# Causal attention scores from 64 contraction rows per head, two heads at a time on the two halves of the PE array's rows

## The chip, the cores and the metric

One core of a Trainium2 chip runs the whole kernel. The time is device microseconds of that core; the kernel before took a median of 586.83 us over three runs (585.6 to 587.18). Where this text speaks of an engine: PE is the matrix engine, DVE the vector engine, ACT the scalar engine, POOL the general-purpose engine, SP the queue from which the transfers are issued.

## The reference

A batch of 256 tokens of 512 numbers goes through three layers, each added to its input:

```python
z = sigmoid((LN(x) Wq^T + bq) (ctx Wk^T + bk)^T / sqrt(128))   # 256 x 25088, no softmax
x = x + z (ctx Wv^T + bv)
c = LN(x) W_kv_down                                            # 256 x 128
k, v, q = heads(c W_k_up), heads(c W_v_up), heads(LN(x) W_q)   # 16 heads of 32
s = (q k^T + rot(LN(x) W_q_rope) rot(c W_k_rope)^T) / 8        # the rotary part is shared by all heads
x = x + concat(softmax(causal(s)) v) W_o
x = x + sum over 8 experts of one_hot * (relu(x wg)^2 * (x wu)) wd
```

The score of a head is thus a product over 64 numbers: 32 that belong to the head and 32 rotary ones that all heads share.

## The kernel before

The first layer streams 25088 context rows in 49 chunks; it takes the first 480 us or so of the span, and the change does not touch its code. What follows, called the section here, is written as small functions that are called in one hand-written list (from L582 on). The suffix or argument `tt` is the half of the tokens (0 or 1, 128 each), `u` a unit of scores, `P` is 128.

For each half: `N1` and `X` normalise and transpose the tokens; `QR` makes the rotary queries, `CKV` the compressed keys and values, `KR` the rotary keys, `K` the heads' keys, `VS` the values, `Q` (four parts) the heads' queries. `S` makes one unit of scores: the matmuls into one PSUM bank of 128x512, the causal mask added by a bf16 matmul with an identity, then a row maximum on DVE (`mx`) and one exponential per head on ACT (`pr`), which also sums the row. `PT` transposes a unit's weights on PE and copies them on DVE (`pt`), `PV` multiplies them with the values, `R1` and `R2` bring the reciprocal sums into shape, `AT` scales and splits, `WO` is the output projection; then `N2` and `Y` normalise and transpose for the experts, and `GU`, `GE`, `IT`, `DN` are the experts' steps.

The scores of two heads come from one matmul over all 128 rows. `kbd` holds the keys as a block pattern: the keys of head `j` of a group of four lie on rows 32j to 32j+31 of column block `j`, the rotary keys on the other half's rows, and the rest is zero, set by POOL (L307). `qs` holds two variants of the queries, each with one half of a group's heads on 64 rows and the rotary queries on the first 32 rows of the other half; it too is zeroed by POOL first (L581). For tt=0 a unit is one group of four heads (two matmuls of 256 columns); for tt=1 it is two heads (one matmul of 512 columns).

All of this is float32; a float32 matmul shows as two weight loads and two matmul records. The order on each engine is the order of the calls: `in_order` (L35) chains every PE, ACT, DVE and POOL instruction to the one before it on its engine, so that nothing is moved by a scheduler. Three buffer rings matter here: the banks of PSUM (`bank`, six), the buffers of the exponentials (`pr`, tag "wr", two) and those of the transposed weights (`pt`, tag "z", two).

Of the kernel before, what the change touches and what calls it, by code (L numbers as in the profile page):

```python
# [11 lines left out]
F32 = mybir.dt.float32  # L12
F32R = mybir.dt.float32r
BF16 = mybir.dt.bfloat16
AF = mybir.ActivationFunctionType
ALU = mybir.AluOpType
AX = mybir.AxisListType
# [3 lines left out]
P = 128  # L21
T = 256
D = 512
KD = D // P
# [24 lines left out]
def body(ctx, tc, a, out, nch=NCH):  # L49
    nc = tc.nc  # L50
    mm = nc.tensor.matmul
    copy, vcopy, tt2 = nc.scalar.copy, nc.vector.tensor_copy, nc.vector.tensor_tensor

    sm = ctx.enter_context(tc.tile_pool(name="sm", bufs=1))
    sb = ctx.enter_context(tc.tile_pool(name="sb", bufs=1))
# [19 lines left out]
    def bank(name):  # L75
        return psum.tile([P, D], F32, tag="b", name=name, bufs=6)
# [4 lines left out]
    def toks(t):  # L81
        return slice(t * P, (t + 1) * P)
# [30 lines left out]
    mask = sm.tile([P, P], BF16, name="mask")  # L113
# [3 lines left out]
    identb = sm.tile([P, P], BF16, name="identb")  # L117
# [25 lines left out]
    rT, rN, sT, sN, kp, zz = {}, {}, {}, {}, {}, {}  # L143
# [101 lines left out]
    ps = bank("qp_ps")[:, :T]  # L245
# [17 lines left out]
    for c in range(nch):  # L263
# [28 lines left out]
        if c >= 4 and plain:  # L292
            n = plain.pop()
# [8 lines left out]
    oh, ol = pair("o", [P, KD, T], "oh")  # L302
    xn = [None, None]

    kbd = [sb.tile([P, 2, 4, T], F32, tag="rT", name=f"kbd{i}", bufs=2) for i in range(2)]
    for i in range(2):
        nc.gpsimd.memset(kbd[i], 0.0)  # L307
    sums = sm.tile([P, 2, NH], F32, name="sums")


# [41 lines left out]
    def prod(ps, tt, w):  # L352
        for j in range(KD):
            mm(ps, lhsT=w(j), rhs=xT[tt][:, j, :], start=j == 0, stop=j == KD - 1)
# [7 lines left out]

    ckv, qr = [None] * 2, [None] * 2

    def CKV(tt):
        ps = bank(f"ckv_ps{tt}")[:, 0:P]
        prod(ps, tt, lambda j: pw["wkvd"][:, toks(j)])
        ckv[tt] = sb.tile([P, P], F32, name=f"ckv{tt}")
        copy(ckv[tt], ps)

    def QR(tt):
        ps = bank(f"qr_ps{tt}")[0:64, 0:P]
        prod(ps, tt, lambda j: pw["wqr"][:, 64 * j:64 * (j + 1)])
        qr[tt] = sb.tile([32, P], F32, name=f"qr{tt}")
        rotated("q", qr[tt], ps, tt)
        for i, r in enumerate((64, 0)):
            nc.vector.tensor_scalar(qs[r:r + 32, tt, i], qr[tt][:, None, :].broadcast_to([32, KD, P]), 0.125, None, ALU.mult)

    def KR(tt):
        ps = bank(f"kr_ps{tt}")[0:64, 0:P]  # L380
        mm(ps, lhsT=pw["wkr"], rhs=ckv[tt], start=True, stop=True)
        kr = sb.tile([32, P], F32, tag="kr", name=f"kr{tt}")
        rotated("k", kr, ps, tt)
        for r in (64, 0):
            for h in range(2):
                (vcopy if h else copy)(kbd[h][r:r + 32, :, 2 - r // 32:4 - r // 32, toks(tt)],
                                       kr[:, None, None, :].broadcast_to([32, 2, 2, P]))

    def K(tt):
        for h in range(2):  # L390
            ps = bank(f"k_ps{tt}{h}")[:, :2 * P].rearrange("p (g t) -> p g t", g=2)
            for g in range(2):
                mm(ps[:, g, :], lhsT=pw["wku"][:, toks(2 * h + g)], rhs=ckv[tt], start=True, stop=True)
            for j in range(4):
                r = slice(32 * j, 32 * j + 32)
                (vcopy if h else copy)(kbd[h][r, :, j, toks(tt)], ps[r])

    def VS(tt):
        ps = bank(f"vs_ps{tt}")
        mm(ps, lhsT=ckv[tt], rhs=pw["wvu"], start=True, stop=True)  # L400
        copy(vs[tt], ps)

    qps = [None, None]

    def Q(tt, g):
        if g == 0:
            qps[tt] = bank(f"q_ps{tt}").rearrange("p (g t) -> p g t", g=KD)
        prod(qps[tt][:, g, :], tt, lambda j: pw["wq2"][:, j * D + g * P:j * D + (g + 1) * P])
        if g == KD - 1:
            for i in range(2):  # L410
                r = slice(64 * i, 64 * i + 64)
                nc.scalar.activation(qs[r, tt, i], qps[tt][r], AF.Copy, scale=0.125)


    pv = [None, None]
    pr, pt = {}, {}

    def heads(tt, u):
        return (u, 0, 4) if tt == 0 else (u // 2, 2 * (u % 2), 2)

    def S(tt, u):
        g, h0, n = heads(tt, u)
        nk = P * (tt + 1)
        p3 = bank(f"s{tt}_{u}").rearrange("p (h k) -> p h k", h=n)
        if tt == 0:
            mm(p3, lhsT=identb, rhs=mask[:, None, :].broadcast_to([P, n, P]), start=True, stop=False)
        for h in range(h0, h0 + n, 2):
            mm(p3[:, h - h0:h - h0 + 2, :], lhsT=qs[:, tt, h // 2, g, :], rhs=kbd[g // 2][:, g % 2, h:h + 2, :nk],  # L428
               start=tt == 1, stop=tt == 0 and h == 2)
        if tt == 1:  # L430
            mm(p3[:, :, P:], lhsT=identb, rhs=mask[:, None, :].broadcast_to([P, n, P]), start=False, stop=True)
        mx = sm.tile([P, 4], F32, tag="mx", name=f"mx{tt}_{u}", bufs=4)
        nc.vector.tensor_reduce(mx[:, :n], p3, AX.X, ALU.max, negate=True)
        pr[tt, u] = sb.tile([P, D], F32, tag="wr", name=f"pr{tt}_{u}", bufs=2).rearrange("p (h k) -> p h k", h=n)
        for i in range(n):
            h = 4 * g + h0 + i
            nc.scalar.activation(pr[tt, u][:, i, :], p3[:, i, :], AF.Exp, bias=mx[:, i:i + 1],
                                 accum_out=sums[:, tt, h:h + 1])

    def PT(tt, u):  # L440
        n = heads(tt, u)[2]
        ps = bank(f"pt{tt}_{u}")
        for i in range(n):
            for kt in range(tt + 1):
                nc.tensor.transpose(ps[:, toks(i * (tt + 1) + kt)], pr[tt, u][:, i, toks(kt)], ident)  # L445
        pt[tt, u] = sb.tile([P, D], F32, tag="z", name=f"pt{tt}_{u}", bufs=2)
        vcopy(pt[tt, u], ps)

    def PV(tt, u):
        g, h0, n = heads(tt, u)  # L450
        if u == 0:
            pv[tt] = psum.tile([P, KD, P], F32, tag=f"acc{tt}", name=f"pv{tt}")
        for i in range(n):
            r = slice(32 * (h0 + i), 32 * (h0 + i + 1))
            for kt in range(tt + 1):
                mm(pv[tt][r, g, :], lhsT=vs[kt][:, g * P + r.start:g * P + r.stop],  # L456
                   rhs=pt[tt, u][:, toks(i * (tt + 1) + kt)], start=kt == 0, stop=kt == tt)
# [3 lines left out]
    def R1(tt):  # L461

        r = sm.tile([P, NH], F32, tag="r", name=f"r{tt}")
        nc.vector.reciprocal(r, sums[:, tt, :])
        rT2[tt] = tmp(f"rx{tt}")
        vcopy(rT2[tt].rearrange("p (h d) -> p h d", h=NH), r[:, :, None].broadcast_to([P, NH, 32]))
# [6 lines left out]
    def AT(tt):  # L473
        at = tmp(f"at{tt}").rearrange("p (g t) -> p g t", g=KD)
        tt2(at, pv[tt], rT2[tt], ALU.mult)
        att[tt] = [t.rearrange("p (g t) -> p g t", g=KD) for t in pair(f"at{tt}", [P, D], "at")]
        split(*att[tt], at)
# [13 lines left out]
    def Y(tt):  # L491
        ps = transposed(bank(f"xc_ps{tt}"), xn[tt])
        split(yhl[0][:, :, toks(tt)], yhl[1][:, :, toks(tt)], ps)
        yT[tt] = sb.tile([P, KD, P], F32, tag=f"xT{tt}", name=f"yT{tt}")
        copy(yT[tt], ps)
# [21 lines left out]
    def GU(tt, e, i, alone=False):  # L517
        if i == 0 or alone:
            gps[tt, e, i] = bank(f"gu{tt}_{e}_{i}").rearrange("p (e w) -> p e w", e=2)
        gps[tt, e, 1] = gps[tt, e, i]  # L520
        w = gu[e + i]
        for j in range(KD):
            s = slice(2 * j * P, 2 * (j + 1) * P)
            mm3(gps[tt, e, i][:, i, :], yhl[0][:, j, toks(tt)], yhl[1][:, j, toks(tt)], w[:, 0, s], w[:, 1, s],
                j == 0, j == KD - 1)
# [39 lines left out]
    ps = bank("rows_ps")  # L565
# [12 lines left out]
    AV1(len(late))  # L578
    o1 = O1(1)
    qs = sb.tile([P, 2, 2, KD, P], F32, tag="N0", name="qs", bufs=2)  # L580
    nc.gpsimd.memset(qs, 0.0)  # L581
    for e, tag in ((5, "N0"), (6, "N1"), (7, "N1")):  # L582
        load_gu(e, tag, 2)
    for e in range(4, E):
# [15 lines left out]
    for i in range(2):  # L600
        nc.sync.dma_start(f(wo[i]), spill["wo"][:, i * KD * D:(i + 1) * KD * D])
    S(0, 0)
    S(0, 1)
    QR(1)
    CKV(1)
    PT(0, 0)
    S(0, 2)
    KR(1)
    K(1)
    PV(0, 0)  # L610
    PT(0, 1)
    Q(1, 0)
    S(0, 3)
    Q(1, 1)
    R1(0)
    VS(1)
    PT(0, 2)
    PV(0, 1)
    PT(0, 3)
    Q(1, 2)  # L620
    Q(1, 3)
# [4 lines left out]
    PV(0, 3)  # L626
    R2(0)
    S(1, 0)
    S(1, 1)
    AT(0)  # L630
    S(1, 2)
    PT(1, 0)
    S(1, 3)
    PT(1, 1)
    WO(0)
    PV(1, 0)
    PV(1, 1)
    PT(1, 2)
    S(1, 4)
    S(1, 5)  # L640
    PV(1, 2)
    N2(0)
    PT(1, 3)
    S(1, 6)
    PT(1, 4)
    Y(0)
    S(1, 7)
    PV(1, 3)
    PV(1, 4)
    PT(1, 5)  # L650
    PT(1, 6)
    GU(0, 0, 0)
    PV(1, 5)
    PT(1, 7)
    R1(1)
    GU(0, 0, 1)
# [114 lines left out]
```

## Time and profile before

| | us |
|---|---|
| median of the timed runs | 586.83 |
| the profiled execution's own time | 586.28 |
| its span (first to last instruction) | 584.5 |
| PE busy | 570.6 (98%) |
| DVE busy | 459.7 (79%) |
| ACT busy | 395.1 (68%) |
| POOL busy | 21.1 (4%) |

The page of the profile lists busy time per engine, a picture of the span in 40 slices, the chain of work that ended last, and groups of instructions with their mean duration and the idle time ahead of them. The answers of the trace give single instructions in order of time. [...] the step from one start to the next says what it costs in a row of matmuls. Times within the run are microseconds from the start of the span.

### The profile page before, as it was taken

The page shows a single profiled execution, that of the slowest core. Times are in us where ns is not written, and L with a number is a line of the kernel's source. Part 1 is how long each engine was busy: PE and PEld are TensorE (multiplying, and loading weights), DVE is VectorE, ACT ScalarE, POOL GpSimd, SP SyncE. Part 2 cuts the span into 40 slices and gives each one's busy share as a digit, 9 for nine tenths or more (in the row PEclk, how much of TensorE's full clock was granted, in tenths as well). Part 3 has the DMA queues.
Part 4 walks back from the last instruction along what each step waited for, and adds up shares of the span by engine and source line. Part 5 has one row for each costly group of instructions (what it writes and reads, how often), then busy time and mean ns, then how long its engine had stood idle before and what let it go on. Part 6 is the DMA issues. An engine that isn't in the chain of part 4 may idle for free.

```text
span 584.5 us, 8061 instructions
## 1 busy us (share of the span) xinstructions
PE 570.6 (98%) x3036; PEld 481.7 (82%) x3036; DVE 459.7 (79%) x528; ACT 395.1 (68%) x512; POOL 21.1 (4%) x28
## 2 busy tenths in 40 slices
PE   4999999999999999999999999999999999999997
PEld 3888888888888888888888888888888887876996
DVE  6898888888888888888888888787878765667543
ACT  5877777777777777777777776767676752574211
POOL 5200000000000000000000000000000041000000
PEclk9999999999999999999999999999999999999999
DMA  8897887879888888788988887565657477700000
GB/s 288 334 368 283 278 295 281 321 278 317 287 324 276 325 271 325 266 337 298 332 282 319 274 337 245 208 225 206 234 198 243 149 295 262 316 1 1 1 1 36
DMA packets 33526, 144.94 MB, mean 248 GB/s; under 512 B 4240, under 2 KB 4432, under 8 KB 19792
## 3 DMA queue, kind: packets, MB, share of 16 engines
q1 hardware_dynamic: 33488, 144.44, 69.3%
q8 instruction: 23, 0.38, 0.2%
q14 instruction: 15, 0.12, 0.1%
HBM read 129.22 MB, written 15.20 MB: 247 GB/s over the span
## 4 chain that ended last, share of the span: by engine, by line
PE 95%; DVE 3%; DMA 1%; issue 0%; POOL 0%; ACT 0%; SPq 0%; POOLq 0%
PE acc L68 15%; PE acc L69 15%; PE acc L70 15%; PE kp_ps L70 8%; PE kp_ps L69 8%; PE kp_ps L68 8%; PE sc L70 4%; PE sc L69 4%; PE sc L68 4%; PE s L428 2%; PE gu L68 1%; PE gu L69 1%; PE gu L70 1%; PE pt L445 1%; DMA wq_r<-in_wq 1%; PE pv L456 1%
## 5 line engine op out<-in xcount | busy, mean ns | idle before, releaser
L68 PE MATMUL acc<-N,z 128*128 128x512 f32 x392 | 153.9, 393 | 0.0
L69 PE MATMUL acc<-N,z 128*128 128x512 f32 x392 | 153.7, 392 | 0.0
L65 DVE TENSOR_TENSOR N<-rN,N 128x2048 fp32r<-128x2048 f32 (+1 forms) x53 | 111.6, 2110 | 52.3 <-ACT N L64 52.2
L70 PE MATMUL acc<-N,z 128*128 128x512 f32 x392 | 152.5, 389 | 0.0
L65 DVE TENSOR_TENSOR T<-rT,T 128x2048 fp32r<-128x2048 f32 (+1 forms) x49 | 110.3, 2252 | 15.3 <-ACT T L64 15.3
L187 ACT ACTIVATE z<-sc 128x512 f32<-128x512 f32 x98 | 58.7, 599 | 66.5 <-PE sc L70 66.2
L64 ACT CAST N<-rN 128x2048 fp32r<-128x2048 f32 (+1 forms) x55 | 94.4, 1725 | 6.1
L64 ACT CAST T<-rT 128x2048 fp32r<-128x2048 f32 (+1 forms) x55 | 94.3, 1721 | 0.9 <-DMA rT<-in_ctxT 0.7
L70 PEld LDWEIGHTS acc<-N,z 128*128 128x128 f32 x392 | 73.6, 188 | 16.0
L68 PEld LDWEIGHTS acc<-N,z 128*128 128x128 f32 x392 | 74.0, 189 | 12.3
L69 PEld LDWEIGHTS acc<-N,z 128*128 128x128 f32 x392 | 74.0, 189 | 11.7
L68 PE MATMUL kp_ps<-T,wk 128*128 128x512 f32 x196 | 76.9, 392 | 0.0
L70 PE MATMUL kp_ps<-T,wk 128*128 128x512 f32 x196 | 76.7, 392 | 0.0
L69 PE MATMUL kp_ps<-T,wk 128*128 128x512 f32 x192 | 74.7, 389 | 0.0
L189 DVE TENSOR_TENSOR zacc<-zacc,z 128x512 f32<-128x512 f32 x98 | 67.2, 686 | 3.7 <-ACT z L187 1.7
L65 DVE TENSOR_TENSOR z<-z,z 128x512 fp32r<-128x512 f32 x98 | 67.3, 686 | 0.0
L64 ACT CAST z<-z 128x512 fp32r<-128x512 f32 x98 | 61.0, 623 | 3.1
L178 ACT ACTIVATE kp<-kp_ps,bk 128x512 fp32r<-128x512 f32 x49 | 33.9, 691 | 39.9 <-PE kp_ps L70 39.9
L70 PE MATMUL sc<-qp,kp 128*128 128x256 f32 x196 | 55.8, 285 | 0.1
L69 PE MATMUL sc<-qp,kp 128*128 128x256 f32 x196 | 55.4, 283 | 0.0
L68 PE MATMUL sc<-qp,kp 128*128 128x256 f32 x196 | 54.9, 280 | 0.0
L68 PEld LDWEIGHTS kp_ps<-T,wk 128*128 128x128 f32 x196 | 37.1, 189 | 7.8
(177 smaller groups left out, 658.5 us busy)
## 6 DMA issues: line engine op xcount, KB each, us to landing
rN<-in_ctxN SPq DMA_DIRECT2D x49, 1024.0 KB, 5.7
rT<-in_ctxT SPq DMA_DIRECT2D x47, 1024.0 KB, 5.5
sp_gu<-w_gu SPq DMA_DIRECT2D x32, 256.0 KB, 4.3
gu<-sp_gu SPq DMA_DIRECT2D x8, 1024.0 KB, 6.0
r_gu<-in_gu SPq DMA_DIRECT2D x16, 256.0 KB, 5.7
sp_dn<-w_dn SPq DMA_DIRECT2D x16, 256.0 KB, 4.3
dn<-sp_dn SPq DMA_DIRECT2D x16, 256.0 KB, 6.0
r_dn<-in_dn SPq DMA_DIRECT2D x8, 256.0 KB, 6.1
```

The source lines that it names most:

```text
L64: copy(hi, src)
L65: eng.tensor_tensor(lo, src, f(hi), ALU.subtract)
L68: mm(ps, lhsT=ahi, rhs=bhi, start=first, stop=False)
L69: mm(ps, lhsT=ahi, rhs=blo, start=False, stop=False)
L70: mm(ps, lhsT=alo, rhs=bhi, start=False, stop=last)
L178: nc.scalar.activation(kp[c][0], ps, AF.Identity, bias=bk)
L187: nc.scalar.activation(z, ps, AF.Sigmoid, scale=1.0 / math.sqrt(128.0))
L189: tt2(zacc, zacc, z, ALU.add)
L428: mm(p3[:, h - h0:h - h0 + 2, :], lhsT=qs[:, tt, h // 2, g, :], rhs=kbd[g // 2][:, g % 2, h:h + 2, :nk], start=tt == 1, stop=tt == 0 and h ...
L445: nc.tensor.transpose(ps[:, toks(i * (tt + 1) + kt)], pr[tt, u][:, i, toks(kt)], ident)
L456: mm(pv[tt][r, g, :], lhsT=vs[kt][:, g * P + r.start:g * P + r.stop], rhs=pt[tt, u][:, toks(i * (tt + 1) + kt)], start=kt == 0, stop=kt == tt)
```

## The change

Each head's scores now come from a matmul of their own over 64 rows: its 32 keys and the 32 rotary keys. A group's heads 0 and 1 lie on rows 0 to 63, heads 2 and 3 on rows 64 to 127. A matmul over rows 0 to 63 and one over rows 64 to 127 stand next to each other in the program and write different banks. `S(tt, k)` makes two units in one call: all matmuls of both, then both maxima, then the exponentials of the first unit and of the second. `qs` and the new `ks` (half the size of the two `kbd`) have no zero parts, so the three memsets go. The copies that fill them are cut to 32 rows each and shared between ACT and DVE by `e`, the parity of the head. The list of calls is rewritten for the paired `S`.

```diff
-    kbd = [sb.tile([P, 2, 4, T], F32, tag="rT", name=f"kbd{i}", bufs=2) for i in range(2)]
-    for i in range(2):
-        nc.gpsimd.memset(kbd[i], 0.0)
+    ks = sb.tile([P, 2, KD, T], F32, tag="rT", name="ks", bufs=2)
...
+    sides = [(e, 64 * i + 32 * e) for e in range(2) for i in range(2)]
...
     def QR(tt):
...
-        for i, r in enumerate((64, 0)):
-            nc.vector.tensor_scalar(qs[r:r + 32, tt, i], qr[tt][:, None, :].broadcast_to([32, KD, P]), 0.125, None, ALU.mult)
+        for e, r in sides:
+            rot = slice(r + 32 - 64 * e, r + 64 - 64 * e)
+            src = qr[tt][:, None, :].broadcast_to([32, KD, P])
+            if e:
+                nc.vector.tensor_scalar(qs[rot, tt, e], src, 0.125, None, ALU.mult)
+            else:
+                nc.scalar.activation(qs[rot, tt, e], src, AF.Copy, scale=0.125)
...
     def KR(tt):
...
-        for r in (64, 0):
-            for h in range(2):
-                (vcopy if h else copy)(kbd[h][r:r + 32, :, 2 - r // 32:4 - r // 32, toks(tt)],
-                                       kr[:, None, None, :].broadcast_to([32, 2, 2, P]))
+        for e, r in sides:
+            (vcopy if e else copy)(ks[r + 32 - 64 * e:r + 64 - 64 * e, e, :, toks(tt)],
+                                   kr[:, None, :].broadcast_to([32, KD, P]))
...
     def K(tt):
...
-            for j in range(4):
-                r = slice(32 * j, 32 * j + 32)
-                (vcopy if h else copy)(kbd[h][r, :, j, toks(tt)], ps[r])
+            for e, r in sides:
+                (vcopy if h else copy)(ks[r:r + 32, e, 2 * h:2 * h + 2, toks(tt)], ps[r:r + 32])
...
         if g == KD - 1:
...
-            for i in range(2):
-                r = slice(64 * i, 64 * i + 64)
-                nc.scalar.activation(qs[r, tt, i], qps[tt][r], AF.Copy, scale=0.125)
+            for e, r in sides:
+                if e:
+                    nc.vector.tensor_scalar(qs[r:r + 32, tt, e], qps[tt][r:r + 32], 0.125, None, ALU.mult)
+                else:
+                    nc.scalar.activation(qs[r:r + 32, tt, e], qps[tt][r:r + 32], AF.Copy, scale=0.125)
...
     def heads(tt, u):
-        return (u, 0, 4) if tt == 0 else (u // 2, 2 * (u % 2), 2)
+        k, i = divmod(u, 2)
+        return [4 * g + 2 * i + e for g in ((2 * k, 2 * k + 1) if tt == 0 else (k,)) for e in range(2)]
...
     def S(tt, k):
...
-        for h in range(h0, h0 + n, 2):
-            mm(p3[:, h - h0:h - h0 + 2, :], lhsT=qs[:, tt, h // 2, g, :], rhs=kbd[g // 2][:, g % 2, h:h + 2, :nk],
-               start=tt == 1, stop=tt == 0 and h == 2)
+        for j in range(n):
+            for i in range(2):
+                g, h = divmod(hs[i][j], 4)
+                r = slice(64 * i, 64 * i + 64)
+                mm(p3[i][:, j, :], lhsT=qs[r, tt, h % 2, g, :], rhs=ks[r, h % 2, g, :nk],
+                   start=tt == 1 and j == 0, stop=tt == 0 and j == n - 1)
...
     qs = sb.tile([P, 2, 2, KD, P], F32, tag="N0", name="qs", bufs=2)
-    nc.gpsimd.memset(qs, 0.0)
```

`PT` and `PV` take their heads from `heads(tt, u)` too. The list of calls from the first `S` to the first expert step, before and after:

```text
before: S(0,0) S(0,1) QR(1) CKV(1) PT(0,0) S(0,2) KR(1) K(1) PV(0,0) PT(0,1) Q(1,0) S(0,3) Q(1,1) R1(0) VS(1)
        PT(0,2) PV(0,1) PT(0,3) Q(1,2) Q(1,3) PV(0,2) PV(0,3) R2(0) S(1,0) S(1,1) AT(0) S(1,2) PT(1,0) S(1,3)
        PT(1,1) WO(0) PV(1,0) PV(1,1) PT(1,2) S(1,4) S(1,5) PV(1,2) N2(0) PT(1,3) S(1,6) PT(1,4) Y(0) S(1,7)
        PV(1,3) PV(1,4) PT(1,5) PT(1,6) GU(0,0,0) PV(1,5) PT(1,7) R1(1) GU(0,0,1)
after:  S(0,0) QR(1) CKV(1) PT(0,0) KR(1) K(1) PT(0,1) S(0,1) PV(0,0) PV(0,1) Q(1,0) Q(1,1) PT(0,2) VS(1) R1(0)
        PT(0,3) Q(1,2) Q(1,3) PV(0,2) PV(0,3) R2(0) S(1,0) AT(0) S(1,1) PT(1,0) PT(1,1) WO(0) PV(1,0) PV(1,1)
        PT(1,2) PT(1,3) S(1,2) PV(1,2) N2(0) PV(1,3) S(1,3) Y(0) PT(1,4) PT(1,5) GU(0,0,0) PV(1,4) PV(1,5)
        PT(1,6) PT(1,7) R1(1) GU(0,0,1)
```

From `GU(0,0,1)` on the two lists are the same, as they are ahead of `S(0,0)`.

More of the change, by code (lines that the diff above doesn't have):

```diff
@@ L418, in heads, with S @@
     def heads(tt, u):
-        return (u, 0, 4) if tt == 0 else (u // 2, 2 * (u % 2), 2)
-    def S(tt, u):
-        g, h0, n = heads(tt, u)
+        k, i = divmod(u, 2)
+        return [4 * g + 2 * i + e for g in ((2 * k, 2 * k + 1) if tt == 0 else (k,)) for e in range(2)]
+    def S(tt, k):
         nk = P * (tt + 1)
-        p3 = bank(f"s{tt}_{u}").rearrange("p (h k) -> p h k", h=n)
+        units = (2 * k, 2 * k + 1)
+        hs = [heads(tt, u) for u in units]
+        n = len(hs[0])
+        p3 = [bank(f"s{tt}_{u}").rearrange("p (h k) -> p h k", h=n) for u in units]
@@ L425, in S @@
         if tt == 0:
-            mm(p3, lhsT=identb, rhs=mask[:, None, :].broadcast_to([P, n, P]), start=True, stop=False)
-        for h in range(h0, h0 + n, 2):
-            mm(p3[:, h - h0:h - h0 + 2, :], lhsT=qs[:, tt, h // 2, g, :], rhs=kbd[g // 2][:, g % 2, h:h + 2, :nk],
-               start=tt == 1, stop=tt == 0 and h == 2)
-        if tt == 1:
-            mm(p3[:, :, P:], lhsT=identb, rhs=mask[:, None, :].broadcast_to([P, n, P]), start=False, stop=True)
-        mx = sm.tile([P, 4], F32, tag="mx", name=f"mx{tt}_{u}", bufs=4)
@@ L433, in S @@
[L433 to L438, printed above, removed]
+            for i in range(2):
+                mm(p3[i], lhsT=identb, rhs=mask[:, None, :].broadcast_to([P, n, P]), start=True, stop=False)
@@ new lines, in S @@
+        for j in range(n):
+            for i in range(2):
+                g, h = divmod(hs[i][j], 4)
+                r = slice(64 * i, 64 * i + 64)
+                mm(p3[i][:, j, :], lhsT=qs[r, tt, h % 2, g, :], rhs=ks[r, h % 2, g, :nk],
+                   start=tt == 1 and j == 0, stop=tt == 0 and j == n - 1)
+        if tt == 1:
+            for i in range(2):
+                mm(p3[i][:, :, P:], lhsT=identb, rhs=mask[:, None, :].broadcast_to([P, n, P]), start=False, stop=True)
+        for i, u in enumerate(units):
+            mx = sm.tile([P, 4], F32, tag="mx", name=f"mx{tt}_{u}", bufs=4)
+            nc.vector.tensor_reduce(mx[:, :n], p3[i], AX.X, ALU.max, negate=True)
+            pr[tt, u] = sb.tile([P, D], F32, tag="wr", name=f"pr{tt}_{u}", bufs=2).rearrange("p (h k) -> p h k", h=n)
+            for j, h in enumerate(hs[i]):
+                nc.scalar.activation(pr[tt, u][:, j, :], p3[i][:, j, :], AF.Exp, bias=mx[:, j:j + 1],
+                                     accum_out=sums[:, tt, h:h + 1])
@@ L440, in PT @@
     def PT(tt, u):
-        n = heads(tt, u)[2]
+        n = len(heads(tt, u))
         ps = bank(f"pt{tt}_{u}")
@@ L449, in PV @@
     def PV(tt, u):
-        g, h0, n = heads(tt, u)
         if u == 0:
             pv[tt] = psum.tile([P, KD, P], F32, tag=f"acc{tt}", name=f"pv{tt}")
-        for i in range(n):
-            r = slice(32 * (h0 + i), 32 * (h0 + i + 1))
+        for i, h in enumerate(heads(tt, u)):
+            g = h // 4
+            r = slice(32 * (h % 4), 32 * (h % 4) + 32)
             for kt in range(tt + 1):
@@ L602, in body @@
     S(0, 0)
-    S(0, 1)
     QR(1)
@@ L606, in body @@
     PT(0, 0)
-    S(0, 2)
     KR(1)
     K(1)
+    PT(0, 1)
+    S(0, 1)
     PV(0, 0)
-    PT(0, 1)
+    PV(0, 1)
     Q(1, 0)
-    S(0, 3)
     Q(1, 1)
+    PT(0, 2)
+    VS(1)
     R1(0)
-    VS(1)
-    PT(0, 2)
-    PV(0, 1)
     PT(0, 3)
@@ L628, in body @@
     S(1, 0)
+    AT(0)
     S(1, 1)
-    AT(0)
-    S(1, 2)
     PT(1, 0)
-    S(1, 3)
     PT(1, 1)
@@ L638, in body @@
     PT(1, 2)
-    S(1, 4)
-    S(1, 5)
+    PT(1, 3)
+    S(1, 2)
     PV(1, 2)
     N2(0)
-    PT(1, 3)
-    S(1, 6)
+    PV(1, 3)
+    S(1, 3)
+    Y(0)
     PT(1, 4)
-    Y(0)
-    S(1, 7)
-    PV(1, 3)
+    PT(1, 5)
+    GU(0, 0, 0)
     PV(1, 4)
-    PT(1, 5)
+    PV(1, 5)
     PT(1, 6)
-    GU(0, 0, 0)
-    PV(1, 5)
     PT(1, 7)
```

## The prediction

> **What bounds the kernel now.** First the page: busy times, then the chain of work that ended last.
>
> ```profile
> PE 570.6 (98%) x3036; PEld 481.7 (82%) x3036; DVE 459.7 (79%) x528; ACT 395.1 (68%) x512; POOL 21.1 (4%) x28
> PE 95%; DVE 3%; DMA 1%; issue 0%; POOL 0%; ACT 0%; SPq 0%; POOLq 0%
> ```
>
> PE is the bound, and 95% of the chain. A saving counts if PE is left without gaps; a gap counts in full. Then busy times in the section, from the stretches (columns: us; then busy us and instructions of PE, weight loads, DVE, ACT, POOL; PE clock; DMA).
>
> ```profile
> 505.00:521.17 16.17, 16.17 (x134) 13.07 (x132) 10.86 (x24) 10.90 (x44) 0.00 (x0) 1.00 0.20 82
> 521.17:540.02 18.85, 18.85 (x134) 11.98 (x133) 13.59 (x23) 10.53 (x37) 0.55 (x1) 1.00 0.00 1
> ```
>
> PE has no gap in 35 us, while ACT and DVE are busy for 55 to 75% of it. The old list keeps every result of theirs ready just ahead of its matmul, with little to spare: a shorter PE part moves PE into their waits. Last, the prices, from the groups of the section (busy us, mean ns of one) and single instructions.
>
> ```profile
> L437 ACT ACTIVATE pr<-s,mx 128x128 f32<-128x128 f32 x16 | 5.6, 372 | 3.4 <-DVE mx L433 3.4
> L386 ACT COPY kbd<-kr 32x512 f32<-32x512 f32 x4 | 2.5, 618 | 1.7 <-DVE kr L361 1.6
> L412 ACT ACTIVATE qs<-q_ps 64x512 f32<-64x512 f32 x4 | 2.4, 592 | 4.8 <-PE q_ps L354 4.7
> L396 DVE COPY kbd<-k_ps 32x256 f32<-32x256 f32 x8 | 3.4, 420 | 0.1
> 509.69 0.30 ACT L369 COPY ckv<-ckv_ps 128x128 f32<-128x128 f32 x1
> 536.05 0.58 ACT L64 CAST y<-xc_ps 128x512 fp32r<-128x512 f32 x1
> 489.55 1.81 POOL L581 MEMSET qs<- 128x2048 f32 x1
> 489.64 2.00 DVE L134 TENSOR_SCALAR xb<-x,mvb,rsb 128x512 f32<-128x512 f32 x1 [0.67 <-POOL rsb L129]
> 502.91 0.54 DVE L134 TENSOR_SCALAR xb<-x,mvb,rsb 128x512 f32<-128x512 f32 x1 [0.67 <-POOL rsb L129]
> 491.69 0.66 PE L139 MATMUL xb_ps<-ident,xb 128*128 128x128 f32 x4 [1.18 <-DVE xb L134]
> ```
>
> Copies on 32 rows cost what those on 64 or 128 do: length sets the price. And the same normalisation takes 2.00 us beside the memset, 0.54 us later; PE waits 1.18 us for it.
>
> [...] No row tile runs before; of the column tiles in `PV` eight records step through in 0.36 us (45 ns each, against 111 ns of `Q`'s), so tiles do overlap. [...]
>
> **The change part by part.** *Score matmuls.* A pair of old tt=0 units steps 2.14 us on PE (504.93 to 507.07, mask 0.22 and 0.86 each), a tt=1 pair 1.94 (521.17 to 523.11). Columns per head stay. If halves overlap, products of a pair take 0.86 us, not 1.72; masks stay (0.43 and 0.22). Two mode switches per call are not in the trace; between nothing and 0.1 us each (around `PV`, steps of 0.49 to 0.53 stand where 0.44 is the least), I take 0.1 to 0.2 per call. So 1.4 and 1.25 us; over two and four calls 7.8 against 12.0: 4.2 us saved. [...]
>
> *Memsets.* That of `qs` gone lets `X(0)` start at 490.51, when PE is free: 1.18 us saved. Those of `kbd` ran at 476 to 480 beside DVE work at its usual 0.69 us: nothing.
>
> *Copies.* `QR` puts two more on ACT (2 x 0.62), `Q` two on DVE (32x512 from PSUM: 0.69, then 0.6; rows of 128x512 take 0.69). In the built program DVE's two of `Q` wait for ACT's second, since both read one bank: `qs` is complete 2.5 us after `Q`, where it took 1.2. `KR` and `K` keep their numbers. SP's order is unchanged; no transfer is added.
>
> *The walk.* I go through the new order with these durations; "after" is where the same work is done.
>
> | point on PE | before | after | what PE waits for |
> |---|---|---|---|
> | `X(0)` starts | 491.69 | 490.51 | nothing |
> | `KR(0)` starts | 495.56 | 495.45 | `ckv` copy behind two `QR` copies: 1.07 |
> | `X(1)` starts | 503.60 | 503.31 | nothing (an old 0.18 gap closes) |
> | `PT(0,0)` starts | 509.19 | 508.8 | second query variant (DVE until 505.97) inside `S(0,0)`: about 0.7 |
> | `KR(1)` starts | 510.80 | 511.8 | `ckv` copy: 2.6 |
> | `Q(1,2)` starts | 518.22 | 520.6 | `PV(0,1)` for `pt`: 1.0 |
> | two tt=1 units done | 523.11 | 526.0 | `qs`, DVE until 525.1: 1.2 |
> | `WO(0)` starts | 525.84 | 529.4 | exponentials, then `at`: 1.2 and 0.2 |
> | `GU(0,0,1)` starts | 540.02 | 544.9 | `pt` at `PV(1,3)`: 0.5; `y`: 2.25 and 0.4 |
>
> `KR(1)`: the maximum starts at 506.8; 0.7, eight exponentials at their 0.343 us step (2.74), two `QR` copies (1.24), `ckv` (0.3) give 511.8; PE has only `QR`, `CKV`, `PT(0,0)` for that time. Before, `S(0,2)` stood there and `ckv` followed the exponentials directly. `PV(0,1)`: its `pt` copy stands on DVE behind `KR` and `K` copies (0.85 + 1.72) that come a microsecond later now. `WO(0)`: `at` needs both maxima of `S(1,0)` first, and on ACT four exponentials. `GU(0,0,0)`: both maxima and four exponentials of `S(1,3)` now stand ahead of the cast of `y`; `mx` from 537.7, exponentials 538.75 to 540.65 (the first waits for its `pr` buffer, `PT(1,4)`), cast to 541.2, DVE's half to 541.95, while PE is through with `PT(1,5)` at 539.0. Before, one unit stood behind `y` instead.
>
> From `GU(0,0,1)` on the lists are equal and PE was never idle: the +4.9 us stay to the end. Against this execution's 586.28 (span 584.5 and 1.78 around it) that is 591.2; on the median, 0.55 above it, 591.7. As a check: the waits of the table sum to 11.1 us, the savings to 5.6 (4.2, 1.18, and other small ones); their difference, 5.5, is within a little over half a microsecond of the walk.
>
> **The rivals.** *Halves don't overlap* (weight loads and products in one line; for it: no row tile is in the trace; against: `PV`'s columns). Then each `S` is 0.86 us longer, but `S(0,1)` and `S(1,0)` hide it under waits for `pt` and `qs`; `S(0,0)` shows half, the last two calls most: 2 us, 593.7. *Gaps cost clock*: PE idles twice for over 2 us, and if the granted clock, 1.00 throughout, were halved afterwards for as long as those gaps last, some 5 us, 2.5 us come on top: 594. The section before has no gap of that size, so its trace says nothing on it. *Faster*: the chain at `KR(1)` and `y` is shorter than I make it. One mechanism: ACT drains a pair's exponentials and copies sooner than its rows say. With all waits hidden the savings alone give 586.8 - 5.6 = 581.2; it decides once the 11 us of waits shrink below 5.6, so ACT's and DVE's steps would have to cost about half of 0.343 and 0.62. The rows vary by a few per cent, which speaks against it. *It evens out* between: 587.
>
> **How the numbers follow.** Walk as it stands 0.66; no overlap 0.13; clock 0.08; evens out 0.07; faster 0.06. The walk has some thirty hand-overs of 0.05 to 0.15 us, and a wait can be off by half a microsecond: its own range is 589.5 to 593.7. With the first two rivals: 589 to 594.6. Within 0.3% (1.76 us) is what a measurement of this kernel can't tell from no change. Slower 0.86, same 0.08, faster 0.06.
>
> **What would show it.** Right: score matmuls of form 64*128, pairs starting within one another; the first `xb` at 0.54 us; PE idle for about 2.6 us ahead of `KR(1)` (for ACT's `ckv`), 1 us at `PV(0,1)`, 1.2 at the first tt=1 unit, 2.25 at the first `gu`. Wrong: gaps missing at `KR(1)` or `y`; score steps not halved; or a clock under 1.00 behind a gap.

## The result: 1.1% slower, and the profile after

The changed kernel takes a median of 592.62 us (592.11 to 593.17), the kernel before, on the same chip, 586.22 us (585.48 to 587.18). The ratio is 1.0112, with a 95% interval of 1.01 to 1.0124. Forecast were 591.7 us and a range of 589.0 to 594.6.

The profiled execution of the changed kernel took 592.99 us, its span is 591.2. First the page: busy times, the clock that PE was granted in 40 slices, and the chain that ended last.

```profile
PE 573.3 (97%) x3068; PEld 483.6 (82%) x3068; DVE 459.8 (78%) x532; ACT 397.4 (67%) x516; POOL 16.0 (3%) x25
PEclk9999999999999999999999999999999999898999
PE 94%; ACT 2%; DVE 2%; DMA 1%; issue 0%; SPq 0%; ACTq 0%
```

PE has become busier, 573.3 us against 570.6, although its score products were cut; two of the 40 slices show a clock below full; and ACT, which had no share of the chain, now has 2% of it, some 12 us. Next, PE's own line through the section (columns: start, length, engine, line, operation, tiles; in brackets the idle time before it and what ended it).

```profile
489.99 0.39 PE L139 MATMUL xb_ps<-ident,xb 128*128 128x128 f32 x2
...
494.99 0.43 PE L386 MATMUL kr_ps<-ckv,wkr 128*64 128x128 f32 x2 [1.10 <-ACT ckv L369]
...
511.60 0.43 PE L386 MATMUL kr_ps<-ckv,wkr 128*64 128x128 f32 x2 [2.55 <-ACT ckv L369]
...
523.88 2.33 PE L441 MATMUL s<-ks,qs 64*128 64x256 f32 x8
526.14 0.39 PE L445 MATMUL s<-mask,identb 128*128 128x256 bf16 x2
526.46 1.14 PE L441 MATMUL s<-ks,qs 64*128 64x256 f32 x8
527.53 0.39 PE L445 MATMUL s<-mask,identb 128*128 128x256 bf16 x2
...
541.63 0.39 PE L68 MATMUL gu<-gu,y 128*128 128x256 f32 x1 [2.11 <-ACT y L64]
...
542.35 0.39 PE L70 MATMUL gu<-gu,y 128*128 128x256 f32 x1 [0.22 <-DVE y L65]
```

`X(0)` follows the streaming part without a gap. Then come the three waits for ACT, of which two are over 2 us: `KR(1)` and the first expert step. The two lines of 64*128 are the new score products of one call each. The second one, from 526.46 to 527.53, waits for nothing: 1.07 us for eight records; the first waits inside for the queries and takes 2.26. Records overlap (in the kernel before those of `Q` last 275 ns on the mean and start 111 ns apart), so a call is counted from its start to the next one's.

The same in stretches around the two long gaps (busy us and instructions of PE, weight loads, DVE, ACT, POOL; PE clock; DMA).

```profile
509.12:512.53 3.41, 0.94 (x7) 0.77 (x8) 1.34 (x4) 2.36 (x9) 0.00 (x0) 1.00 0.00 0
512.53:515.95 3.42, 3.42 (x18) 2.52 (x18) 3.25 (x9) 2.69 (x6) 0.00 (x0) 0.50 0.02 5
539.83:543.25 3.42, 1.40 (x9) 1.20 (x10) 1.64 (x3) 2.33 (x8) 0.00 (x0) 1.00 0.00 0
543.25:546.66 3.41, 3.41 (x28) 2.80 (x27) 0.63 (x2) 0.00 (x0) 0.00 (x0) 0.50 0.02 5
```

After each of the two long gaps the clock is 0.50 for 3.4 us and then full again. Averaged over stretches of 4 us, which the experiments below use, that is 0.63 (513 to 517), 0.78 (541 to 545) and 0.79 (545 to 549). In the kernel before it was 1.00 in the whole section.

What ACT was doing while PE waited for `ckv` and for `y`:

```profile
509.99 1.27 ACT L382 ACTIVATE qs<-qr 32x512 f32<-32x512 f32 x2
511.28 0.27 ACT L369 COPY ckv<-ckv_ps 128x128 f32<-128x128 f32 x1
...
540.53 0.48 ACT L451 ACTIVATE pr<-s,mx 128x256 f32<-128x256 f32 x1
...
540.98 0.60 ACT L64 CAST y<-xc_ps 128x512 fp32r<-128x512 f32 x1
```

It did what the forecast had it do: two rotary copies ahead of `ckv`, and the exponentials of `S(1,3)` right up to the cast of `y`.

### The profile page after: what moved, and what is told of

The parts are those of the page before. It is cut to its first block, busy times and chain, and to the rows that moved or that the text cites. A ratio compares the mean times of both kernels' runs of the same rounds, so it can differ in the third digit from the quotient of the medians.

```text
span 591.2 us, 8128 instructions
## 1 busy us (share of the span) xinstructions
PE 573.3 (97%) x3068; PEld 483.6 (82%) x3068; DVE 459.8 (78%) x532; ACT 397.4 (67%) x516; POOL 16.0 (3%) x25
## 4 chain that ended last, share of the span: by engine, by line
PE 94%; ACT 2%; DVE 2%; DMA 1%; issue 0%; SPq 0%; ACTq 0%
PE acc L68 15%; PE acc L69 15%; PE acc L70 15%; PE kp_ps L68 8%; PE kp_ps L69 8%; PE kp_ps L70 8%; PE sc L70 4%; PE sc L69 4%; PE sc L68 4%; PE gu L70 1%; PE gu L68 1%; PE gu L69 1%; PE q_ps L352 1%; PE s L441 1%; ACT pr L451 1%; PE pt L459 1%
```

## The experiments

Three theories had to be told apart. (1) *Waits of the order*: the halves overlap and save time, but ACT and DVE deliver late in the new order. (2) *Clock*: the idle time itself is bad, since PE runs slower after it. (3) *No overlap*: the new products are no cheaper. A fourth question was whether the part of the change that is nothing but the memset gives all the gain there is.

Because the streaming part ends up to 2 us earlier or later from one execution to the next (the first product of `X(0)`, where PE doesn't wait for it, at 488.79 to 490.96), each kernel also has the length of the section, from PE's first product of `X(0)` to its first of `R2(1)`, in its profiled execution.

| kernel | median, us | ratio to before, 95% | section, us |
|---|---|---|---|
| before (586.08, 585.92, 586.35 and 586.67 beside the later kernels) | 586.22 | 1 | 50.53 |
| changed | 592.62 | 1.0112 (1.01 to 1.0124) | 58.91 |
| before, memset of `qs` on DVE | 584.81 | 0.9978 (0.9972 to 0.9985) | 50.48 |
| changed, `CKV(1)` first | 590.64 | 1.0083 (1.0066 to 1.01) | 57.56 |
| changed, `Y(0)` ahead of `S(1,3)` | 590.79 | 1.008 (1.0065 to 1.0095) | 56.45 |
| changed, gaps filled | 591.16 | 1.0088 (1.0073 to 1.0103) | 57.05 |
| changed, halves in turn | 592.56 | 1.0107 (1.0083 to 1.013) | 58.94 |
| changed, rotary copies on POOL | 590.51 | 1.008 (1.0062 to 1.0097) | 55.96 |
| rewoven | 586.85 | 1.0021 (1.0012 to 1.003) | 53.18 |
| rewoven, rotary copies on POOL | 590.07 | 1.0066 (1.0053 to 1.0079) | 54.87 |
| rewoven, copies later | 590.05 | 1.0061 (1.0045 to 1.0076) | 56.10 |
| before, memset on DVE, again | 584.64 | 0.9974 (0.9963 to 0.9984) | 50.46 |
| rewoven, first copies later | 586.75 | 1.0 (0.999 to 1.001) | 52.60 |

The 1.18 us that PE waited ahead of `X(0)` in the kernel before lie outside the section. So the changed kernel's section is 8.38 us longer, of which the missing gap gives 1.18 back, and the streaming part ended 0.52 earlier in its profiled execution: 6.68, the difference of the spans (591.2 and 584.5).

**The memset alone, in the kernel before.**

```diff
-    nc.gpsimd.memset(qs, 0.0)
+    nc.vector.memset(qs, 0.0)
```

> The kernel before, with one edit: the queries' buffer is zeroed by DVE behind the first normalisation, not by POOL beside it. [...] the first normalisation falls from 2.00 to about 0.55 us, PE's gap of 1.18 us ahead of its transposes goes, and the time falls by 1.2 us (ratio 0.998). DVE has 2.5 us free behind it, so its own memset (1 to 2 us) costs nothing. Rival, that the 2.00 us have another cause: no change.

584.81 us, 0.9978: 1.3 us less. In this kernel's lines the normalisation takes 0.55 us, where it took 2.00 beside POOL's memset, and `X(0)` follows at once:

```profile
489.44 0.55 DVE L134 TENSOR_SCALAR xb<-x,mvb,rsb 128x512 f32<-128x512 f32 x1 [0.67 <-POOL rsb L129]
490.36 1.76 DVE L581 MEMSET qs<- 128x2048 f32 x1 [0.37 <-issue]
```

The memset takes 1.76 us on DVE (1.81 on POOL before), but behind `xb`, where nothing waits for it. So the one part of the change whose gain reaches the end can be had without the rest.

**`CKV(1)` ahead of the scores, in the changed kernel.**

```diff
+    CKV(1)
     S(0, 0)
     QR(1)
-    CKV(1)
     PT(0, 0)
```

> The changed kernel with one call moved: CKV(1) stands ahead of S(0,0), so that the copy of the compressed keys comes ahead of the eight exponentials and the two rotary copies on ACT. Theory of the waits: PE's gap of 2.55 us ahead of KR(1) goes, a new one of about 0.5 us stands ahead of CKV(1), the clock of the stretch behind (0.63) is back at 1.00, and 2 us are gained as long as later waits don't take them back: 590.6 (ratio to before 1.007). Rival, that the score matmuls on half the rows are what costs: no change, 592.6.

590.64 us, as theory 1 said: 2 us less, not the 2.55 of the gap. The gap at `KR(1)` is gone, and PE's line has waits in three other places instead, the longest at `PV(0,1)`:

```profile
503.54 1.16 PE L352 MATMUL ckv_ps<-xT,wkvd 128*128 128x128 f32 x8 [0.41 <-ACT xT L348]
...
507.49 1.37 PE L459 MATMUL pt<-ident,pr 128*128 128x128 f32 x4 [0.25 <-ACT pr L451]
508.80 0.43 PE L386 MATMUL kr_ps<-ckv,wkr 128*64 128x128 f32 x2
...
514.13 0.63 PE L470 MATMUL pv<-pt,vs 128*32 128x128 f32 x8 [1.29 <-DVE pt L461]
```

This wait at `PV(0,1)` stood in the forecast's table, with 1.0 us, but not in the changed kernel's trace. There the clock of 0.63 had stretched PE's work ahead of it until `pt` was there. Here PE keeps its clock, and the wait shows.

**`Y(0)` ahead of `S(1,3)`.**

```diff
+    N2(0)
     S(1, 2)
     PV(1, 2)
-    N2(0)
     PV(1, 3)
-    S(1, 3)
     Y(0)
+    S(1, 3)
```

> The changed kernel with N2(0) moved ahead of S(1,2) and Y(0) ahead of S(1,3), so that the cast of y stands ahead of the last four exponentials on ACT. Theory of the waits: PE's gap of 2.11 us ahead of the first expert product goes, and with it the low clock behind (0.78): 3.5 to 4 us gained, 588.9 (ratio 1.0045). Rival, that only the clock counts: 1.4 us gained, 591.2. Rival, that the half-row matmuls cost: no change.

590.79 us, between the two and nearer to the 591.2 of the clock: 1.8 us less, 2.5 in the section. The 2.11 at `gu` is gone, and the clock is 1.00 from 537 to 549. In PE's line two short waits are left there:

```profile
540.27 0.39 PE L70 MATMUL gu<-gu,y 128*128 128x256 f32 x1 [0.22 <-DVE y L65]
...
542.06 1.24 PE L470 MATMUL pv<-pt,vs 128*32 128x128 f32 x16 [0.33 <-DVE pt L461]
```

In the trace both are gone, the gap and the low clock behind it, and a part of both comes back as new waits for `pt`: 0.33 us ahead of `PV(1,4)`, and 0.6 inside, since the two `PV` take 1.16 us (0.60 in the next kernel, where they don't wait). How the gain divides between gap and clock this run alone does not say.

**The two gaps filled with products.** Ahead of `KR(1)` and of the first expert step PE makes products that the real ones overwrite: more is computed than needed, nothing is left out.

```diff
     def KR(tt):
-        ps = bank(f"kr_ps{tt}")[0:64, 0:P]
+        full = bank(f"kr_ps{tt}")
+        for _ in range(2 * tt):
+            mm(full, lhsT=pw["wvu"][:, 0:P], rhs=pw["wvu"], start=True, stop=True)
+        ps = full[0:64, 0:P]
...
+        for j in range(16 if (tt, e, i) == (0, 0, 0) else 0):
+            mm(gps[tt, e, i][:, 0, :], lhsT=w[:, 0, 0:P], rhs=w[:, 0, 0:2 * P], start=True, stop=True)
```

> The changed kernel with products put into its two long gaps on PE, into banks that the next products overwrite: 1.7 us of them ahead of KR(1), 1.9 us ahead of the first expert product. Nothing else waits for them. If the low clock behind the gaps comes of the idle time, the clock stays at 1.00 and about 1.4 us are gained behind the second gap, little behind the first, where a later wait hides it: 591 (ratio 1.0085). If the low clock has another cause: no change, 592.6. The gaps as waits stay in both.

591.16 us, 1.4 us less though PE does more. The stretches that had a clock of 0.63, 0.78 and 0.79, with this kernel's columns as above:

```profile
513.00:517.00 4.00, 3.29 (x39) 2.47 (x39) 3.83 (x10) 2.68 (x6) 0.00 (x0) 1.00 0.01 4
...
541.00:545.00 4.00, 3.58 (x38) 2.84 (x37) 1.89 (x3) 1.38 (x4) 0.00 (x0) 1.00 0.01 4
545.00:549.00 4.00, 4.00 (x46) 3.67 (x45) 1.97 (x5) 0.59 (x1) 0.00 (x0) 1.00 0.00 0
```

The clock stays full in the whole section. The waits for ACT are still there in substance, since the products only sit in them (0.83 us are left at `KR(1)`, and 0.71 now shows at `PV(0,1)`). So the idle time lowers the clock here (0.63, 0.78 and 0.79 with it, 1.00 without), and the two low stretches together are worth about 1.4 us in the medians of four runs each, 1.9 in the sections of the two traces. This separates theory 2 from theory 1: the clock is a real part of the loss, and the smaller one.

**Halves in turn.** All products of rows 0 to 63 first, then those of rows 64 to 127.

```diff
-        for j in range(n):
-            for i in range(2):
+        for i in range(2):
+            for j in range(n):
```

> The changed kernel with the two loops of its score matmuls exchanged: all matmuls on rows 0 to 63 first, then all on rows 64 to 127, so that neighbours in the program no longer lie on different halves. If neighbours must lie on different halves to overlap, the eight products of a tt=1 call take about 1.7 us where they took 1.07, and of the added 0.65 us per call about 2 us in all reach the end, the rest being hidden under the waits for qs and pt: 594.6 (ratio 1.0145). If PE pairs them whatever their order, or never overlapped them, the call keeps its 1.07 us and the time its 592.6.

592.56 us, no difference: the expectation was missed. A call at full clock takes, in PE's line, just as long as in the changed kernel:

```profile
526.23 1.14 PE L441 MATMUL s<-ks,qs 64*128 64x256 f32 x8
527.30 0.39 PE L445 MATMUL s<-mask,identb 128*128 128x256 bf16 x2
```

1.07 us again. In both kernels the single records of this call start in pairs, about a hundredth of a microsecond apart, in four steps: in the changed kernel at 526.46, 526.78, 527.00 and 527.21, in this one at 526.23, 526.55, 526.77 and 526.98. A step of 0.22 is what one record of an old product of 256 columns took (0.86 for four). So two records do run side by side, which settles theory 3.

They belong to products on different halves, not to the two records of one product. `S(1,0)`, whose queries come late one after the other, shows it. In the changed kernel its first product has its two records at 523.88 and 524.20, and the second product, on the other half, at 524.06 and 524.38. In this kernel the first product runs alone, and the second and the third start together when the query copy that the second needs is there; in the list they are the last of one half and the first of the other:

```profile
524.55 0.49 PE L441 MATMUL s<-ks,qs 64*128 64x256 f32 x2 [0.21 <-DVE qs L415]
```

Once nothing waits, the four products of a tt=1 call pair up in either order. With more of one half in front the order does count: in a tt=0 call, with eight records of rows 0 to 63 ahead, the first record of the other half starts only behind the start of the fifth (504.93 in `S(0,0)`, which began at 504.37, and 515.23 in `S(0,1)`, which began at 514.21). `S(0,1)` took 2.17 us here and 1.45 in the changed kernel, each partly at the low clock. In the time of the kernel that loss is not seen; the wait at `KR(1)` is 2.08 us here instead of 2.55. One of the four runs of this kernel kept a mean clock of 1.000 and took 589.93 us, where the others, at 0.993 or 0.994, took 592.43 to 593.97. That points to a price of 2.5 us for the low clock, but single runs are a hint only: one run of the changed kernel had a mean clock of 0.999 and took 592.25, no less than its others.

**Rotary query copies on POOL instead of ACT.**

```diff
-                nc.scalar.activation(qs[rot, tt, e], src, AF.Copy, scale=0.125)
+                nc.gpsimd.tensor_scalar(qs[rot, tt, e], src, 0.125, None, ALU.mult)
```

> The changed kernel with the two copies of the rotary queries that it put on ACT moved to POOL, and nothing else. Theory of the waits: the gap of 1.10 us ahead of KR(0) goes, that ahead of KR(1) falls from 2.55 to about 1.3 us and the low clock behind it goes; the gap at y with its low clock stays. 1.1 us surely, 1 us more if the wait for pt at PV(0,1) does not take it back: 590.7 (ratio 1.008). Rival, that ACT's copies are covered by the exponentials anyway: no change.

590.51 us, as theory 1 had it: no wait at `KR(0)`, and 1.22 instead of 2.55 at `KR(1)`. With 1.22 the clock stayed at 1.00. It has a price of its own, two copies in 3.46 us on POOL (ACT: 1.27), and PE waits for `xb` at `X(1)`. PE's line first:

```profile
501.70 0.63 PE L139 MATMUL xb_ps<-ident,xb 128*128 128x128 f32 x4 [0.62 <-DVE xb L134]
...
508.58 0.43 PE L386 MATMUL kr_ps<-ckv,wkr 128*64 128x128 f32 x2 [1.22 <-ACT ckv L369]
```

POOL's line of the same kernel:

```profile
492.92 3.46 POOL L382 TENSOR_SCALAR qs<-qr 32x512 f32<-32x512 f32 x2 [4.18 <-PE ckv_ps L352]
```

**Rewoven.** The moves of `CKV(1)`, `N2(0)` and `Y(0)` shown above, and two more: `QR(0)` behind `CKV(0)` and `O2`, and `PV(0,1)` behind two parts of `Q`, with `VS(1)` last.

```diff
-    QR(0)
     CKV(0)
     O2(1, o1)
+    QR(0)
     KR(0)
...
     PV(0, 0)
-    PV(0, 1)
     Q(1, 0)
     Q(1, 1)
+    PV(0, 1)
     PT(0, 2)
-    VS(1)
+    Q(1, 2)
     R1(0)
     PT(0, 3)
-    Q(1, 2)
     Q(1, 3)
+    VS(1)
```

> The changed kernel with its list of calls rewoven and nothing else: CKV(0) and the transposes of O2(1) ahead of QR(0), CKV(1) ahead of S(0,0), PV(0,1) behind Q(1,1), Q(1,2) and Q(1,3) earlier, N2(0) ahead of S(1,2) and Y(0) ahead of S(1,3). Theory of the waits: from 592.6, about 0.5 at KR(0), 2 at KR(1), 1.3 at PV(0,1), 0.8 at the first tt=1 call and 1.9 at y are gained if they add up: 586.1, level with the kernel before (ratio 1.000). Rival, that each gap closed opens another one behind it: 589.

586.85 us, ratio 1.0021: 5.8 us less than the changed kernel with the same products. The clock is 1.00 in every stretch of the section. So the greater part of the loss, 5.7 of the 8.4 us of section, was the order's. The longest wait that is left in PE's line is of DVE's making:

```profile
502.40 0.63 PE L139 MATMUL xb_ps<-ident,xb 128*128 128x128 f32 x4 [1.18 <-DVE xb L134]
```

DVE has 0.85 us of `QR(0)` copies between its other work and the normalisation, now that `QR(0)` comes later.

**Rewoven, with the copies on POOL.** The two edits shown above, together.

> As the rewoven list, and with the rotary queries' two copies on POOL too. The theory of the waits gives another 0.5 us at KR(0) and up to 1 us at KR and K of the second half, as ACT is free for their copies earlier: 585 (ratio 0.998). If POOL's copies are slow (over 2 us each) or hold up DVE's[...]: no gain over the rewoven list, or a loss.

590.07 us, 3.2 us more than without POOL; the rival was right. In the profiled executions the section is 1.7 us longer (54.87 against 53.18), and the streaming part ended 1.4 us later; whether that part of the 3.2 us has to do with POOL is not shown. DVE's copies become slow as long as POOL is at its own (two `QR` copies in 1.17 us instead of 0.85, two `KR` copies in 1.60 instead of 0.85), and `X(1)` waits twice as long:

POOL's line, and then PE's:

```profile
496.27 3.27 POOL L382 TENSOR_SCALAR qs<-qr 32x512 f32<-32x512 f32 x2 [5.99 <-PE k_ps L397]
```

```profile
504.85 0.63 PE L139 MATMUL xb_ps<-ident,xb 128*128 128x128 f32 x4 [2.24 <-DVE xb L134]
```

What DVE loses beside POOL differs, as far as POOL's spans, which are rough, can be trusted. In the kernel before, the normalisation took 2.00 us beside a memset of 1.81 and ended 0.28 behind it (491.64 and 491.36). Here the second `QR(0)` copy on DVE starts at 496.54, beside a POOL copy that runs from 496.27 to 497.89, and ends at 497.28; it took 0.74 us instead of 0.42, but it did not wait for POOL's end. And three DVE products of 32x128 from 497.29 on, beside POOL's two copies (496.27 to 499.54), keep their 0.28 each. Which work of DVE is slowed, and by what, is not shown. In this execution the gap of 2.24 left the clock at 1.00.

**Rewoven, copies later.** The rotary query copies become a call of their own, `QC`, and are put behind `N1(1)` and `PV(0,1)`; `Q(1,2)` and `Q(1,3)` go one call ahead of `PT(0,2)` and `PT(0,3)`. Against the rewoven kernel:

```diff
         rotated("q", qr[tt], ps, tt)
+
+    def QC(tt):
         for e, r in sides:
...
     N1(1, v1)
+    QC(0)
...
     PV(0, 1)
+    QC(1)
+    Q(1, 2)
     PT(0, 2)
-    Q(1, 2)
     R1(0)
-    PT(0, 3)
     Q(1, 3)
+    PT(0, 3)
     VS(1)
```

> The rewoven order, with two more moves: the copies of the rotary queries become a call of their own (QC), QC(0) behind N1(1), QC(1) behind PV(0,1); and Q(1,2) and Q(1,3) each go one call ahead of PT(0,2) and PT(0,3). In the rewoven kernel PE waits 1.18 us at X(1) for DVE, which has 0.85 us of rotary copies ahead of the normalisation, and PT(0,2) takes 1.34 us instead of 0.6 because its exponentials come late. Theory that the half-row scores are good and only the order of the copies loses time: 0.85 less at X(1) (a gap of 0.3 is left) and 0.7 less at PT(0,2), 1.5 us in all: 585.3 us, ratio 0.999. Rival that each wait taken away opens one behind it (the copies now stand ahead of Q's in ACT's and DVE's lines, and S(0,0) or S(1,0) waits for them): 586.8, ratio 1.002.

590.05 us: 3.2 more than the rewoven kernel, worse than either theory. Up to `Q(1,2)` it ran ahead as meant (the gap at `X(1)` is 0.35). Then, in DVE's line and in PE's:

```profile
519.53 1.39 DVE L417 TENSOR_SCALAR qs<-q_ps 32x512 f32<-32x512 f32 x2 [1.61 <-ACT qs L419]
520.95 0.69 DVE L463 COPY pt<-pt 128x512 f32<-128x512 f32 x1
```

```profile
521.70 1.07 PE L472 MATMUL pv<-pt,vs 128*32 128x128 f32 x8 [2.38 <-DVE pt L463]
```

DVE's copies of `Q(1,3)` wait for ACT, and the copy of `pt` stands behind them; PE is out of work for 2.38 us, and over the next 4 us the clock averages 0.58.

**Rewoven, first copies later**, and the memset on DVE once more. `QC(1)` directly behind `QR(1)` and `Q(1,3)` behind `PT(0,3)`, as in the rewoven kernel; `QC(0)` behind `N1(1)` and `Q(1,2)` ahead of `PT(0,2)` are kept.

> The second rewoven kernel with one fault mended: there Q(1,3) had gone ahead of PT(0,3), its DVE copies waited for ACT's rotary and query copies, and the copy of pt for PT(0,3) stood behind them, so that PV(0,3) waited 2.38 us and the clock fell to 0.58 after it. Here QC(1) follows QR(1) directly as in the first rewoven kernel, Q(1,3) stands behind PT(0,3) again, and only QC(0) behind N1(1) and Q(1,2) ahead of PT(0,2) are kept. Theory that the waits were all of the order's making: 0.85 us at X(1) and 0.5 at PT(0,2) and PT(0,3) less than the first rewoven kernel, 585.5 us, ratio 0.9985, no clock under 1.00. Rival that at this density any move opens another wait: 586.8 or more, ratio 1.001.

> The kernel before with the memset of qs on DVE instead of POOL, once more, beside the second rewoven kernel on the same chip: 584.8 us, ratio 0.998. Whether the half-row scores are worth anything over this one edit is read from the two.

586.75 us, ratio 1.0 (0.999 to 1.001): the gap at `X(1)` is 0.36, but the section is only 0.58 us shorter than in the rewoven kernel (52.60 against 53.18), where 1.35 was expected. Of the 0.8 us gained at `X(1)`, 0.2 is lost again at once at `CKV(1)`. At `PT(0,2)` and `PT(0,3)` nothing is gained: the two take 1.58 us behind `Q(1,2)`, where they took 1.18 and 0.50 around it. The kernel before with its memset on DVE, which ran beside "copies later", takes 584.64 us this time, its section 50.46. It is the fastest of all, and beats both the kernel before and the changed one.

So the half-row scores, in the best order that I found, cost 2.1 us of section over a kernel without them. Their own saving on PE is 3.2 to 3.7 us (below), so some 5 to 6 us of waits remain in that order. Some 4.7 us can be pointed to: `PT(0,0)` takes 1.31 us and waits another 0.25, where 0.44 would do; the block of `PT(0,2)` and `PT(0,3)` 1.58 instead of 0.87, that of `PT(1,0)` and `PT(1,1)` about 1.9 instead of 1.0; `S(1,0)` loses 0.3, `X(1)` 0.4, `CKV(1)` 0.2, the expert step 0.2, and `PV(1,4)` 0.3 ahead of it and 0.6 inside. The largest, at the `PT` blocks, are waits for exponentials: the transposes there follow one another at the step of ACT's exponentials, 0.35 us a head for tt=0 and 0.46 for tt=1. An order without them was not found; whether there is one is open.

## Why the prediction was right, step by step

**What bounds the kernel**: right. What PE had lost at the point from which the lists are equal stayed lost: from there to the end of the span both kernels take 44.5 us.

**The walk**, with its points as measured:

| point on PE | forecast | measured | |
|---|---|---|---|
| `X(0)` | 490.51 | 489.99 | the streaming part ended 0.52 earlier |
| `KR(0)` | 495.45 | 494.99 | wait 1.10, forecast 1.07 |
| `X(1)` | 503.31 | 502.83 | |
| `PT(0,0)` | 508.8 | 508.44 | |
| `KR(1)` | 511.8 | 511.60 | wait 2.55, forecast 2.6 |
| `Q(1,2)` | 520.6 | 520.83 | right sum, wrong part |
| two tt=1 units done | 526.0 | 526.46 | |
| `WO(0)` | 529.4 | 529.74 | |
| `GU(0,0,0)` | 541.25 | 541.63 | waits 2.11 and 0.22, forecast 2.25 and 0.4 |
| `GU(0,0,1)` | 544.9 | 546.70 | the clock |

The points fit better than the steps. Counted from `X(0)`, the walk is 0.9 us short at `GU(0,0,0)` (51.64 measured, 50.74 forecast) and 2.3 at `GU(0,0,1)` (56.71 and 54.39); that the streaming part happened to end 0.52 earlier hides a part of it. What is missing ahead of `GU(0,0,0)` fits the score matmuls, which saved less than was forecast, and the low clock behind `KR(1)`.

**Where it was off: the last step.** Between `GU(0,0,0)` and `GU(0,0,1)` the forecast had 3.65 us, and it took 5.07. The waits there were a little shorter than forecast; the work was longer. The clock was 0.50 from 543.25 on, the last products of `gu` stepped at 0.21 us instead of 0.12, `PV` took 1.03 instead of 0.60 and `PT` 1.58 instead of 0.85 (the steps with the gaps filled). The walk priced the clock at nothing. The rival "gaps cost clock" had the mechanism, at 0.08 and 2.5 us, as something in place of the walk; in fact it came with it, and a clock under 1.00 behind a gap stood among the signs of being wrong. On this point the sum was wrong; the range of 589 to 594.6, which took that rival in, covered it. The filled gaps give 1.4 us for both stretches together; since a wait that a slow clock hides comes back with a full one, the clock's effect on PE's work alone is larger: half of 3.41 us, 1.7 us, for each low stretch in which PE is busy throughout (an estimate from the clock of 0.50; behind the second gap, 6.68 us from `GU(0,0,0)` to `PV(1,6)` against 5.15 with the gaps filled). The forecast had read only that the section before had no such gap; it should have given this rival the higher chance.

**`Q(1,2)`**: right in sum for a wrong reason. The wait of 1.0 at `PV(0,1)` is not in the trace, since the slow clock from 512.5 to 516 filled it. With a full clock it appears, with 1.29 (`CKV(1)` first), 0.80 (copies on POOL) and 0.71 (gaps filled).

**Score matmuls**: the mechanism was right, the size was not. Forecast were 1.4 and 1.25 us a call. Where nothing waits, a tt=0 call takes 1.62 us (510.59 to 512.21 with `CKV(1)` first: 0.53 for the masks, 1.09 for 16 records), a tt=1 call 1.40 (526.46 to 527.86). Against 2.14 and 1.94 that saves 2 x 0.52 + 4 x 0.54 = 3.2 us, not 4.2. The two old figures end with a call's last record, the new ones with the start of what comes next; counted to that point in both, the tt=0 units took 4.50 us and take 3.24 in the rewoven kernel, the tt=1 units took 7.94 and take about 5.5 there without the wait in `S(1,0)`, and the saving is 3.7. The surplus per call over half the old products is 0.21 to 0.23 and sits in the first and last step of a call, about 0.1 longer each than the others; the forecast's own estimate of a surplus had an upper end of 0.2, and the value taken was lower. The masks, forecast at 0.43 and 0.22, take up to 0.1 us more too.

**Memset**: right. 1.18 forecast; alone it gave 1.3 us (584.81 against 586.08) and 1.7 (584.64 against 586.35), with ratios of 0.9978 and 0.9974.

**Copies**: right for ACT (`QR` copies 1.27 for two, forecast 1.24) and for DVE's wait for ACT's second copy of `Q` (1.42 and 2.29 us in DVE's line).

**The rivals**: "halves don't overlap" is out, by the pairs of records. "Faster" and "it evens out" are out for this order; the rewoven orders show what they would have needed, all waits under 1.3 us, and even then only 586.75.

**The clock, as the traces show it.** In the changed kernel each stretch of low clock behind a gap has 0.50 and is 3.41 us long, and the starts of the two lie nine of these lengths apart (512.53 and 543.25). They do not start where the gap ends but 0.93 and 1.62 us behind it. The sections of the traces have eight low stretches, and each takes the same from the averages over 4 us, 0.43 in sum from the two that it touches (0.13 and 0.30 for the first one with the halves in turn); that is 1.72 us, half of 3.4. From these averages, with 0.50 for the low clock, the two with the halves in turn start about 30.7 us apart (an estimate), nine lengths again.

Each of the eight stands behind a long gap on PE:

| kernel | gaps with a low clock behind them, us |
|---|---|
| changed | 2.55 and 2.11 |
| changed, `CKV(1)` first | 2.11 |
| changed, `Y(0)` ahead of `S(1,3)` | 2.55 |
| changed, halves in turn | 2.08 and 2.12 |
| changed, rotary copies on POOL | 2.11 |
| rewoven, copies later | 2.38 |

Shorter gaps left the clock at 1.00, the longest of them 1.29 us (`PV(0,1)` with `CKV(1)` first). Where the limit lies between 1.29 and 2.08 no run shows.

One gap does not fit a limit on the length alone: the 2.24 us in the rewoven kernel with copies on POOL, where all averages from 498 to 522 are 1.00. The distances of nine lengths, and the starts up to 1.62 us behind a gap, suggest that idle time is counted in stretches of 3.41 us, one after the other, so that a gap across two of them counts in parts. That is an estimate from these numbers; where such stretches lie in that execution is not shown. Three of that kernel's six runs have a mean clock of 0.996, as the profiled run with the copies on POOL in the changed order has with its one low stretch, and three have 1.000: so this kernel loses clock in some executions and not in others.

What a low stretch costs in time varies. The three runs with 0.996 took 590.03 to 590.27 us, the other three 588.81 to 590.13; with the copies later, the one run with 1.000 took 588.02 us and the other five 589.86 to 590.54.

## What to carry to other kernels

A cheaper operation on the bounding engine is worth its saving only where the engines that feed it can deliver sooner; in a list where every result is ready just in time, read the slack of each hand-over first, since here 3 to 4 us saved on PE came with a section that is 8.4 us longer. Where a result has to be late, keep the gap short or put other work into it: here eight of nine gaps of 2.08 to 2.55 us on PE were paid a second time, in clock, and none of up to 1.29 was. And split a change before judging it: the one part whose gain reached the end, a memset that no longer ran on POOL beside a normalisation on DVE, was worth 0.2% alone and needed nothing of the rest.

## What the runs showed that was not expected

- The clock after idle time: 0.50 for 3.41 us in the changed kernel, then full again, and as much lost behind eight of nine gaps of 2.08 to 2.55 us; 1.00 behind those of up to 1.29.
- A slow clock can hide a wait: the forecast 1.0 us at `PV(0,1)` was not to be seen at 0.50, and appeared with 0.71 to 1.29 when the clock stayed full.
- Products on the two halves of the rows pair up in either order when a call has four: 1.07 us for eight records in both. With eight records of one half in front, the other half's first started only behind the start of the fifth.
- Two copies of 32x512 take 3.2 to 3.5 us on POOL (its spans are rough), 1.27 on ACT and 0.85 on DVE, and DVE's own copies take up to 1.60 while POOL's run.
